# Graph layers on one core: the first unit's copies and scaling on VectorE, its row factors through the sums' banks, x loads behind the adjacency, and new order tables

## The chip, the cores and the metric

The kernel runs on one core of one Trainium2 chip. The metric is the time of one launch on the device, in microseconds. The profiler's span goes from the first to the last instruction of one profiled execution. In the text PE is TensorE, DVE is VectorE, ACT is ScalarE, POOL is GpSimd and SP is SyncE, which issues most of the DMAs.

## The reference, cut to what matters

There are eight batches of 2048 nodes with 128 features, all in float32, and one symmetric adjacency of 2048 x 2048 (about 3% of its entries are set). Each batch passes four layers, and each layer adds its result to x.

```python
h = maximum(layernorm(x), 0); x = x + L0(h)   # and so on for layers 1, 2, 3

# layers 0, 1, 3: graph attention, one head
Wh = h @ W.T                                  # layer 1: h @ W; layer 3: also a layernorm
e = leaky_relu(Wh @ a1 [:, None] + Wh @ a2 [None, :], 0.2)
out = softmax(where(adj > 0, e, -9e15)) @ Wh  # layers 0 and 3: elu at the end

# layer 2: attention of h with itself, four heads of 32
scores = leaky_relu(einsum('bihk,bjhk->bhij', x, x), 0.2)
out = softmax(where(adj == 0, -inf, scores)) @ x
```

## The kernel before, in words

A **unit** is one layer of one batch. Units of layers 0, 1 and 3 are of class `Gat`, those of layer 2 of class `Heads`. All units lie in one instruction stream, in which work of different batches alternates.

A `Gat` unit first makes its rows. The statistics are taken on DVE (L451; for the first unit L482), the reciprocal root by a power on POOL (L111; L488), a bias on DVE (L116; L492), and the scaled and clipped rows on ACT (L511), four quarters of 512 nodes each (q0 to q3). For each quarter PE transposes the rows (L540), ACT copies them out of PSUM (`copy`, L558), PE multiplies by the weights (`project`, L566), and ACT takes the exponentials (`exps`, L595 to L597) and multiplies four blocks by one of them (`put`, L591). The row factors `r` are needed along the free dimension on every partition. For the very first unit, batch 0's layer 0, and two more, `spread` turns them by eight transposes for each half (L650) into one PSUM pair, from where ACT copies them to SBUF (L659). For the other units they pass through DRAM: a turn on PE (L673), a copy, a write (L681) and a broadcast read (L698), both on SP's queue.

The softmax of such a unit is a chain of 32 **tokens**: two halves of its 2048 targets by sixteen blocks of sources. A token is one `front` on DVE (L718: the larger of two factors, times the adjacency) and one `back` on PE (L727: 8 blocks into PSUM, recorded as 16 matmuls). After 16 tokens `out` divides and adds the result to x. All tokens of all units form one chain in the order of the table TOKENS.

A `Heads` unit keeps its rows in DRAM in split form, and loads each head's sources `s`, targets `m` and values `v` (`load`, L928). It then runs 64 **beats**, 16 for each head. A beat is two score pairs on PE (L994), two exponentials on ACT (L1001), one mask on DVE (L1007) and its weighing on PE (L1016).

[...] Banks 4 to 7 are two **pairs**, which scores, transposes, projections and row turns borrow in turn; banks 1 to 3 hold the sums of the tokens (`sums`), and bank 0 the weighed values of the beats.

The adjacency (16 loads of 1 MB, `adjacency`, L366) becomes one byte per entry on DVE (L369, `edge`). `symmetry` (L382, L386 on PE and L392 on ACT) and `verdict` establish that it is symmetric; each of its pieces needs its row and the first unit's values. The loads use the tags `z` (five buffers) and `m` (two). `load_x` (L420) issues the loads of x on SP: batch 0's in four quarters, the others whole.

The order is not written by hand. Each step is an `add` with an engine, a duration, a due time and its needs. `Plan.run` goes through all of them with a model of the engines, and takes, of the steps that could start within WINDOW_US, the one due first; tokens' fronts are moved ahead by HURRY_US while more than one of their buffers is free. The due times come from TOKENS (start and step of each half), BEATS (start and step of each head), LEADS (how long before its start a unit is prepared) and EARLY (a shift for each kind of step). The model's durations affect only the order: each engine then works in that order, and waits for its data by semaphores.

Of the kernel before, what the change touches and what calls it, by code (L numbers as in the profile page):

```python
# [40 lines left out]
def adj_preln_d4(ctx: ExitStack, tc: tile.TileContext, x, adj, w0, a0, w1, a1, w3, a3,  # L41
# [117 lines left out]
    HURRY_US, WINDOW_US, BEAT_SUMS_US = 70.8, 0.139, 0.86  # L159

    EARLY = dict(front=-107.6, score=111.1, exp=-8.6, mask=-164.7, sums=-334.5)
# [78 lines left out]
    def fast(ctx):  # L240
# [117 lines left out]
        rows_in, squares = [], []  # L358

        def adjacency(j):  # L360
            tag, bufs = ("m", 2) if j % 6 > 3 else ("z", 5)
            raw = {}

            def load(op):
                raw[0] = big.tile([P, N], I32, tag=tag, name="raw", bufs=bufs)
                nc.sync.dma_start(out=raw[0], in_=adj[j * P:(j + 1) * P, :])  # L366

            def edges(op):
                nc.vector.tensor_scalar(edge[:, j, :], raw[0], 0.0, EDGE, op0=OP.is_gt, op1=OP.mult)  # L369

            last = add("SP", 2.5, 5.0 + 0.1 * j, load, takes=[tag], lag=5.5)
            rows_in.append(add("DVE", 1.14, 20.0 + 3.0 * j, edges, [last], frees=[(tag, last)]))
# [42 lines left out]
        def load_x(b, due):  # L415
            def load(op):
                X[b] = big.tile([P, NB, C], F32, tag="x", name="x", bufs=4)
                xv = x[b].rearrange("(n p) c -> p n c", p=P)
                for sl in ([slice(0, NB)] if b else [slice(q * 4, q * 4 + 4) for q in range(4)]):
                    nc.sync.dma_start(out=X[b][:, sl, :], in_=xv[:, sl, :])  # L420

            x_taken[b] = add("SP", 2.0, due, load, takes=["x"], lag=17.0 if b else 4.5)
            done[b, 0] = [x_taken[b]]
# [3 lines left out]
        class Unit:  # L427
# [44 lines left out]
            def first_moments(self):  # L472
# [22 lines left out]
                for half in range(2):  # L495
                    last = add("DVE", 1.9, half, lambda op, half=half: stats(op, half), self.after)
                    last = add("POOL", 3.4, half, lambda op, half=half: power(op, half), [last])
                    last = add("DVE", 0.09, half, lambda op, half=half: end(op, half), [last])
                    ready += [last] * 2
# [45 lines left out]
        class Gat(Unit):  # L545
            def beginning(self):
# [4 lines left out]
                ends, self.v_ready = [], []  # L551
                for q in range(4):
# [3 lines left out]
                    def copy(op, q=q, turn=turn):  # L556
                        self.h_t[q] = quarter("h_t")
                        nc.scalar.copy(self.h_t[q], ps[:, turn.got["pair"], :])  # L558

                    copied = add("ACT", 0.47, self.due(part), copy, [turn], frees=[("pair", turn)])  # L560

                    def project(op, q=q):
                        lo = op.got["pair"]
                        pv = ps[:, lo:lo + 2, :].rearrange("p b (k c) -> p (b k) c", c=256)
                        for k in range(4):
# [4 lines left out]
                                  takes=["pair"], frees=[("h_t", turn)])  # L570
                    put = self.put3 if layer == 3 else self.put
# [3 lines left out]
                self.v_ready = ends  # L575
# [8 lines left out]
            def put(self, q, lo):  # L584
# [4 lines left out]
                for k in range(4):  # L589
                    n = q * 4 + k  # L590
                    nc.scalar.activation(self.y[:, n, :C], pv[:, k, :C], AF.Copy, scale=self.y[:, n, C:CE])  # L591
# [46 lines left out]
            def spread(self):  # L638
# [4 lines left out]
                if (self.b, self.layer) in ((0, 0), (0, 1), (B - 1, 3)):  # L643
                    for half in range(2):
                        def turn(op, half=half):
                            lo = op.got["pair"]
                            pk = ps[:, lo:lo + 2, :].rearrange("p b (k t) -> p (b k) t", t=P)
                            for k in range(HB):
# [3 lines left out]
                        turned = add("PE", 0.9, self.due(0.95), turn,  # L652
                                     last if (self.b, self.layer) != (0, 0) else last[half * 2:half * 2 + 2],
                                     takes=["pair", "r"])

                        def copy(op, half=half, turned=turned):
                            self.r[half] = big.tile([P, HN], F32, tag="r", name="r", bufs=2)
                            lo = turned.got["pair"]
                            nc.scalar.copy(self.r[half], ps[:, lo:lo + 2, :].rearrange("p b t -> p (b t)"))  # L659

                        self.r_ready[half] = turned, add("ACT", 0.9, self.due(0.95), copy, [turned],
                                                         frees=[("pair", turned)])
# [28 lines left out]
            def targets(self, half, due):  # L691
# [9 lines left out]
                op = add("SP", 0.5, due, read, [self.written], takes=["r"], lag=7.5)  # L701
# [9 lines left out]
            def token(self, a, due, place, last_front, last_back, first, last, gate=None):  # L711
# [20 lines left out]
                powers = self.powers if self.layer == 3 else self.v_ready[jb // 4]  # L732
# [3 lines left out]
                b = add("PE", 1.8, due, back, [f, last_back, self.v_ready[jb // 4]],  # L736
# [149 lines left out]
        class Heads(Unit):  # L886
# [41 lines left out]
            def load(self, h, due):  # L928
# [7 lines left out]
                def target(op):  # L936
                    self.M[h] = m = big.tile([P, N], F32R, tag="m", name="m")
# [8 lines left out]
                s0 = add("SP", 1.9, due, lambda op: source(op, 0), self.there, takes=["s"], lag=3.0)  # L946
                m = add("SP", 1.0, due, target, self.there, takes=["m"], lag=7.0)
                s1 = add("SP", 1.9, due + 4, lambda op: source(op, 1), self.there, takes=["s"], lag=3.0)
                v = add("SP", 0.5, due, values, self.there, takes=["v"], lag=7.5)
                return s0, s1, m, v  # L950

            def beats(self, heads):
# [4 lines left out]
                for h, (start, step) in enumerate(heads):  # L957
                    ops = self.load(h, start - 24.0)
                    for jb in range(NB):
# [3 lines left out]
                        for c2 in range(2):  # L963
                            score = add("PE", 0.46, due - EARLY["score"] + c2, lambda op, s=s, c2=c2: self.scores(op, s, c2),
# [7 lines left out]
                        if jb == NB - 1:  # L972
                            score.frees.append(("m", ops[2]))
# [88 lines left out]
            (1, 0, 0): (-22.6, 16.91), (0, 1, 0): (53.7, 14.45), (0, 1, 1): (278.3, 12.5),  # L1062
            (1, 0, 1): (1550.7, 12.7), (2, 0, 0): (1538.2, 13.82), (2, 0, 1): (1781.1, 13.31),
            (1, 1, 0): (27.5, 13.73), (1, 1, 1): (467.0, 14.14), (2, 1, 0): (387.8, 14.31),
            (2, 1, 1): (552.8, 14.26), (3, 0, 0): (1505.8, 15.6), (3, 0, 1): (544.1, 12.33),
            (0, 3, 0): (1892.8, 13.82), (0, 3, 1): (1951.1, 14.82), (3, 1, 0): (2559.2, 13.34),
            (4, 0, 0): (1368.4, 13.75), (3, 1, 1): (1830.4, 13.22), (4, 0, 1): (1802.4, 13.44),
            (1, 3, 0): (1217.9, 11.81), (1, 3, 1): (1320.1, 15.08), (4, 1, 0): (1665.0, 14.27),
            (4, 1, 1): (2914.6, 13.92), (5, 0, 0): (1883.5, 13.18), (5, 0, 1): (1527.4, 14.37),
            (2, 3, 0): (1788.0, 14.72), (2, 3, 1): (2978.9, 11.74), (5, 1, 0): (3082.5, 14.35),  # L1070
            (5, 1, 1): (3404.4, 13.78), (6, 0, 0): (3203.1, 14.22), (6, 0, 1): (3460.2, 14.74),
            (3, 3, 0): (3608.3, 13.23), (3, 3, 1): (3684.5, 14.14), (6, 1, 0): (3899.4, 13.51),
            (6, 1, 1): (3952.0, 13.91), (7, 0, 0): (3923.9, 14.06), (7, 0, 1): (4831.6, 11.9),
            (4, 3, 0): (4281.7, 12.22), (7, 1, 0): (3732.3, 17.2), (7, 1, 1): (4400.2, 13.13),
            (4, 3, 1): (4958.4, 13.51), (5, 3, 0): (4812.0, 14.1), (5, 3, 1): (4921.6, 16.9),
            (6, 3, 0): (4366.7, 12.89), (6, 3, 1): (5490.0, 14.47), (7, 3, 0): (4783.0, 17.58),
            (7, 3, 1): (6177.5, 14.4),
        }
        BEATS = {
            (0, 0): (-186.75, 13.08), (0, 1): (-165.33, 21.31), (0, 2): (148.16, 8.98),  # L1080
            (0, 3): (258.71, 2.23), (1, 0): (-691.29, 9.57), (1, 1): (-490.1, 1.76),
            (1, 2): (-690.86, 3.48), (1, 3): (-210.23, 0.0), (2, 0): (88.81, 9.71),
            (2, 1): (97.72, 2.18), (2, 2): (646.55, 10.8), (2, 3): (1293.92, 18.43),
            (3, 0): (-837.42, 3.77), (3, 1): (1119.9, 1.12), (3, 2): (1122.42, 9.21),
            (3, 3): (1398.66, 23.92), (4, 0): (1467.16, 19.39), (4, 1): (2195.99, 8.65),
            (4, 2): (2652.74, 7.66), (4, 3): (3088.57, 11.55), (5, 0): (3462.55, 12.1),
            (5, 1): (3394.91, 8.46), (5, 2): (3605.57, 10.37), (5, 3): (3626.73, 12.28),
            (6, 0): (2736.83, 6.75), (6, 1): (3799.1, 0.43), (6, 2): (3983.93, 8.76),
            (6, 3): (3990.18, 12.29), (7, 0): (2647.8, 4.65), (7, 1): (2776.44, 0.0),
            (7, 2): (3122.04, 3.46), (7, 3): (3703.42, 8.07),  # L1090
        }
        LEADS = {
            (0, 0): 491.95, (1, 0): 357.11, (0, 1): 1280.8, (2, 0): 1208.77, (1, 1): 234.77,
            (3, 0): 828.81, (2, 1): 747.18, (0, 3): 274.58, (3, 1): 427.1, (4, 0): 119.58,
            (1, 3): 1195.59, (4, 1): 1350.06, (5, 0): 313.09, (2, 3): 599.37, (5, 1): 1322.07,
            (6, 0): 552.24, (3, 3): 361.02, (6, 1): 1007.92, (7, 0): 968.09, (4, 3): 325.57,
            (7, 1): 257.23, (5, 3): 781.66, (6, 3): 786.06, (7, 3): 1366.98, (0, 2): 836.12,
            (1, 2): 1588.43, (2, 2): 1046.3, (3, 2): -638.09, (4, 2): -597.43, (5, 2): 978.35,
            (6, 2): -1278.59, (7, 2): 69.8,
# [253 lines left out]
```

## Time and profile before

| | |
|---|---|
| median of 3 runs (lowest to highest) | 2748.1 us (2745.65 to 2750.09) |
| the profiled execution's own time | 2748.61 us |
| its span | 2746.8 us |
| mean granted PE clock in it | 0.993 |
| first adjacency conversion (L369), and the last | 14.38 us, 55.87 us |
| first token on PE (L727) | 35.86 us |
| first score on PE (L994) | 273.50 us |
| one front (L718), one mask (L1007), one exponential (L1001) | 1278, 2285, 1113 ns |

An engine's busy time is the sum of its recorded instructions. Matmuls are pipelined and their ends are modelled, so PE's busy time is no measure of how near it is to its peak; the distance from one start to the next in the timeline is. In a table of stretches the columns are PE, PE's weight loads, DVE, ACT and POOL, each with its count in brackets, then the granted clock, the DMA share and GB/s. In the waits, a line gives the waiting engine and line, what it waited for, the sum in microseconds, the number of times and the longest.

### The profile page before, as it was taken

The numbers are of one execution on the slowest core, as the hardware profiler recorded it, in microseconds if no ns is written. First come the engines' busy times: TensorE is split into PE (matmuls) and PEld (weight loads), VectorE is DVE, ScalarE is ACT, GpSimd is POOL, SyncE is SP. The second block draws the span as 40 slices with busy tenths as digits, with TensorE's granted clock in tenths as the row PEclk, the third lists the DMA queues.
The fourth block names the chain that finished last, engine by engine and source line by source line (L and its number), as shares of the span: only waits on it lengthen the run. The fifth ranks groups of instructions, "written<-read, shape, count | busy, mean of one in ns | idle before, by whom it ended". The sixth has DMA issues, their size and how long they took to land. (4 is left out here: it accounts for less than half of the span.)

```text
span 2746.8 us, 48941 instructions
## 1 busy us (share of the span) xinstructions
PE 2626.4 (96%) x20104; PEld 2020.1 (74%) x20104; DVE 2515.0 (92%) x3323; ACT 1720.2 (63%) x2789; POOL 261.7 (10%) x114
## 2 busy tenths in 40 slices
PE   6999999989998999999999999999999999999987
PEld 6999877757774777867777677786787667565677
DVE  7868899989999899999999999999999899899987
ACT  4333665576567558666767666665676757787651
POOL 2101010011000101111100110010111100011000
PEclk9999999999999999999999999999999999999999
DMA  8003223433323223232323321423225221422000
GB/s 311 17 9 99 64 55 62 93 85 62 62 47 77 55 55 85 55 70 55 67 62 81 78 47 47 103 53 70 55 59 105 47 58 28 108 54 55 13 16 25
DMA packets 212842, 181.80 MB, mean 66 GB/s; under 512 B 142448, under 2 KB 177728, under 8 KB 206464
## 3 DMA queue, kind: packets, MB, share of 16 engines
q1 hardware_dynamic: 144112, 156.46, 21.1%
q0 software_dynamic: 68080, 22.04, 8.0%
q8 instruction: 160, 2.62, 0.4%
q14 instruction: 74, 0.61, 0.1%
q10 hardware_dynamic: 416, 0.07, 0.0%
HBM read 123.03 MB, written 33.73 MB: 57 GB/s over the span
## 5 line engine op out<-in xcount | busy, mean ns | idle before, releaser
L1001 ACT ACTIVATE z<-ps,shift 128x1024 f32<-128x1024 f32 x1024 | 1122.7, 1113 | 727.1 <-PE ps L994 721.4
L727 PEld LDWEIGHTS ps<-y,zg 128*128 128x128 f32 x12288 | 1466.0, 192 | 71.3 <-DVE zg L718 20.0
L727 PE MATMUL ps<-y,zg 128*128 128x129 f32 x12288 | 1497.1, 276 | 15.5 <-DVE zg L718 10.4
L1007 DVE SCALAR_TENSOR_TENSOR z<-z,edge 128x2048 f32<-128x2048 f32 x512 | 1169.3, 2285 | 64.0 <-ACT z L1001 63.2
L718 DVE SCALAR_TENSOR_TENSOR zg<-r,cr,edge 128x1024 f32<-128x1024 f32 x768 | 970.5, 1278 | 98.1 <-PE ps L727 88.0
L994 PE MATMUL ps<-m,s 128*128 128x512 f32 x2048 | 721.1, 438 | 63.6 <-ACT z L1001 59.1
L994 PEld LDWEIGHTS ps<-m,s 128*128 128x128 f32 x2048 | 314.2, 191 | 339.4 <-ACT z L1001 241.1
L1016 PE MATMUL ps<-z,v 128*32 128x512 f32 x4096 | 500.9, 601 | 2.2 <-DVE z L1007 1.6
L1016 PEld LDWEIGHTS ps<-z,v 128*32 128x32 f32 x4096 | 103.5, 109 | 234.4 <-issue 183.3
L511 ACT ACTIVATE h<-x,nmrx,rstdx 128x128 f32<-128x128 f32 x512 | 210.7, 491 | 32.7 <-DVE nmrx L116 18.6
L111 POOL TENSOR_TENSOR rstdx<-varx,neg_half 128x16 f32<-128x16 f32 x31 | 130.3, 4204 | 643.9 <-DVE varx L106 643.9
L1041 POOL DMA_DIRECT2D x<-o x31 | 65.8, 2124 | 906.8 <-DVE o L1036 811.8
L451 DVE BATCH_NORM_STATS2 st<-x 128x6 f32<-128x128 f32 x496 | 106.2, 278 | 0.0
L566 PEld LDWEIGHTS ps<-rhs,h_t 128*128 128x128 f32 x768 | 98.3, 194 | 10.7 <-ACT h_t L558 3.0
L566 PE MATMUL ps<-rhs,h_t 128*128 128x130 f32 x768 | 104.3, 281 | 0.4 <-ACT h_t L558 0.3
L540 PE MATMUL ps<-ident,h 128*128 128x128 f32 x512 | 79.9, 279 | 15.7 <-ACT h L511 10.9
L795 POOL DMA_DIRECT2D x<-oa x26 | 23.4, 901 | 702.3 <-ACT z L1001 189.3
L540 PEld LDWEIGHTS ps<-ident,h 128*128 128x128 f32 x512 | 62.1, 142 | 35.0 <-ACT h L511 13.9
L760 DVE TENSOR_TENSOR oa<-ps,rs 128x384 f32<-128x384 f32 x144 | 73.9, 513 | 5.0
L558 ACT COPY h_t<-ps 128x512 f32<-128x512 f32 x96 | 55.2, 581 | 34.9 <-PE ps L540 34.9
L766 ACT ACTIVATE oe<-oa 128x1024 f32<-128x1024 f32 x32 | 33.8, 1058 | 68.8 <-DVE oa L785 59.2
L591 ACT ACTIVATE y<-ps,y 128x128 f32<-128x128 f32 x256 | 73.0, 369 | 0.0
(123 smaller groups left out, 830.7 us busy)
## 6 DMA issues: line engine op xcount, KB each, us to landing
s<-halves SPq DMA_DIRECT2D x256, 128.0 KB, 2.7
m<-halves SPq DMA_DIRECT2D x64, 512.0 KB, 6.5
r<-row SPq DMA_DIRECT2D x42, 512.0 KB, 3.7
raw<-in_adj_dram SPq DMA_DIRECT2D x16, 1024.0 KB, 16.9
x<-oa POOLq DMA_DIRECT2D x26, 512.0 KB, 4.6
values<-h SPq DMA_DIRECT2D x32, 256.0 KB, 2.2
halves<-hi SPq DMA_DIRECT2D x128, 64.0 KB, 1.7
halves<-lo SPq DMA_DIRECT2D x128, 64.0 KB, 1.7
```

What stands on the lines that cost most here:

```text
L111: nc.gpsimd.tensor_tensor(out=rstd, in0=v, in1=neg_half, op=OP.pow)
L451: nc.vector.bn_stats(out=key["st"][:, n, :], in_=rows()[:, n, :])
L511: nc.scalar.activation(self.h[q][:, k, :], X[self.b][:, n, :], AF.Relu, scale=key["rstd"][:, n:n + 1], bias=key["nmr"][:, n:n + 1])
L540: nc.tensor.transpose(pk[:, k, :], self.h[q][:, k, :], ident)
L566: nc.tensor.matmul(pv[:, k, :C + 2], lhsT=self.h_t[q][:, k * P:(k + 1) * P], rhs=rhs, start=True, stop=True)
L718: nc.vector.scalar_tensor_tensor(z, self.r[half], self.cr[:, 0, jb:jb + 1], edge[:, jb, half * HN:(half + 1) * HN], op0=OP.max, op1=OP.mult)
L727: nc.tensor.matmul(ps[:, self.banks(half, place)[i // 3], k * CE:(k + 1) * CE], lhsT=z[:, i * P:(i + 1) * P], rhs=self.y[:, jb, :], start= ...
L760: nc.vector.tensor_mul(key["a"][:, i0:i1, :], pv[:, :, :C], r[:, i0:i1, None].to_broadcast([P, i1 - i0, C]))
L994: nc.tensor.matmul(ps[:, lo + c, :], lhsT=self.S[h, jb // HB][:, at:at + P], rhs=self.M[h][:, (c2 * 2 + c) * 512:(c2 * 2 + c + 1) * 512], ...
L1001: nc.scalar.activation(self.z[s][:, c2 * HN:(c2 + 1) * HN], ps[:, lo:lo + 2, :].rearrange("p b t -> p (b t)"), AF.Exp, bias=shift)
L1007: nc.vector.scalar_tensor_tensor(self.z[s], self.z[s], 1.0, edge[:, jb, :], op0=OP.mult, op1=OP.mult, accum_out=self.den[:, h, jb:jb + 1])
L1016: nc.tensor.matmul(ps[c * HD:(c + 1) * HD, 0, :], lhsT=self.V[h][:, jb, :], rhs=z[:, c * 512:(c + 1) * 512], start=jb == 0, stop=jb == NB - 1,
```

## The change

For the first unit, batch 0's layer 0, the copies of the transposed rows out of PSUM and the multiplication of the four blocks of each quarter move from ACT to DVE; the multiplication is one instruction for a quarter instead of four. The transposes of its row factors need the exponentials only (`r_made`), no longer the scaled values, and half 0's go through banks 2 and 3 of the sums in place of a pair. The loads of x of the batches 1 to 7 need all adjacency loads in the plan, and so stand behind them on SP. In batch 0's layer 2, the targets of head 1 get a POOL instruction, `hold`, that reads an element of head 0's targets and writes one of head 1's, so that the load of head 1's targets comes after head 0's have landed. Several durations and lags of the model are altered, and TOKENS, BEATS, LEADS, EARLY, HURRY_US and WINDOW_US have new values. Of the sequence of TOKENS, the first eight halves differ in that batch 3's half 0 of layer 0 comes before batch 1's half 1 of layer 1; at the end both halves of batch 7's layer 1 come before batch 5's and 4's layer 3.

```diff
-    HURRY_US, WINDOW_US, BEAT_SUMS_US = 70.8, 0.139, 0.86
-    EARLY = dict(front=-107.6, score=111.1, exp=-8.6, mask=-164.7, sums=-334.5)
+    HURRY_US, WINDOW_US, BEAT_SUMS_US = 194.3, 0.136, 0.86
+    EARLY = dict(front=-260.8, score=238.0, exp=-105.8, mask=-318.7, sums=-441.8)
...
-            last = add("SP", 2.5, 5.0 + 0.1 * j, load, takes=[tag], lag=5.5)
+            last = add("SP", 2.5, 5.0 + 0.1 * j, load, takes=[tag], lag=6.0)
+            loaded.append(last)
...
-            x_taken[b] = add("SP", 2.0, due, load, takes=["x"], lag=17.0 if b else 4.5)
+            x_taken[b] = add("SP", 0.8 if b else 2.8, due, load, loaded[:] if b else (), takes=["x"], lag=17.0 if b else 3.5)
...
-                    last = add("POOL", 3.4, half, lambda op, half=half: power(op, half), [last])
+                    last = add("POOL", 1.7, half, lambda op, half=half: power(op, half), [last])
...
+                    begins = (self.b, layer) == (0, 0)
...
-                        nc.scalar.copy(self.h_t[q], ps[:, turn.got["pair"], :])
-                    copied = add("ACT", 0.47, self.due(part), copy, [turn], frees=[("pair", turn)])
+                        (nc.vector.tensor_copy if begins else nc.scalar.copy)(self.h_t[q], ps[:, turn.got["pair"], :])
+                    copied = add("DVE" if begins else "ACT", 0.61 if begins else 0.47, self.due(part), copy,
+                                 [turn], frees=[("pair", turn)])
...
+                    if begins:
+                        exped.append(add("ACT", 0.45, self.due(part + 0.04), lambda op, q=q, product=product:
+                                         self.put(q, product.got["pair"], False), [product] + exped[-1:]))
+                        ends.append(add("DVE", 0.75, self.due(part + 0.05), lambda op, q=q, product=product:
+                                        self.put_on_vector(q, product.got["pair"]), [exped[-1]],
+                                        frees=[("pair", product)]))
+                        continue
...
-                self.v_ready = ends
+                self.v_ready, self.r_made = ends, exped or ends
...
+            def put_on_vector(self, q, lo):
+                pv = ps[:, lo:lo + 2, :].rearrange("p b (k c) -> p (b k) c", c=256)
+                sl = slice(q * 4, q * 4 + 4)
+                nc.vector.tensor_mul(self.y[:, sl, :C], pv[:, :, :C], self.y[:, sl, C:CE].to_broadcast([P, 4, C]))
...
+                        room = "sums" if (self.b, self.layer, half) == (0, 0, 0) else "pair"
...
-                        turned = add("PE", 0.9, self.due(0.95), turn,
-                                     last if (self.b, self.layer) != (0, 0) else last[half * 2:half * 2 + 2],
-                                     takes=["pair", "r"])
+                        turned = add("PE", 0.9, self.due(0.95 if room == "pair" else 0.5), turn,
+                                     last if (self.b, self.layer) != (0, 0) else self.r_made[half * 2:half * 2 + 2],
+                                     takes=[room, "r"])
...
-                powers = self.powers if self.layer == 3 else self.v_ready[jb // 4]
+                powers = self.powers if self.layer == 3 else self.r_made[jb // 4]
...
-                b = add("PE", 1.8, due, back, [f, last_back, self.v_ready[jb // 4]],
+                b = add("PE", 1.785, due, back, [f, last_back, self.v_ready[jb // 4]],
...
+                if (self.b, h) == (0, 1):
+                    def hold(op):
+                        self.M[h] = big.tile([P, N], F32R, tag="m", name="m")
+                        nc.gpsimd.tensor_copy(self.M[h][0:1, 0:1], self.M[0].bitcast(F32)[0:1, 0:1])
+                    held = add("POOL", 1.0, due, hold, self.first_target, takes=["m"])
+                    self.there, there, m_taken = there + [held], there + [held], []
...
-                            score.frees.append(("m", ops[2]))
+                            score.frees.append(("m", ops[4]))
...
-            (1, 0, 0): (-22.6, 16.91), (0, 1, 0): (53.7, 14.45), (0, 1, 1): (278.3, 12.5),
+            (1, 0, 0): (-73.0, 12.4), (0, 1, 0): (287.7, 12.93), (0, 1, 1): (371.7, 10.73),
...
-            (0, 0): (-186.75, 13.08), (0, 1): (-165.33, 21.31), (0, 2): (148.16, 8.98),
-            (0, 3): (258.71, 2.23), (1, 0): (-691.29, 9.57), (1, 1): (-490.1, 1.76),
+            (0, 0): (-180.01, 6.53), (0, 1): (-578.0, 14.45), (0, 2): (-556.59, 10.52),
+            (0, 3): (-148.64, 9.04), (1, 0): (-1224.04, 11.55), (1, 1): (-933.99, 3.82),
...
-            (0, 0): 491.95, (1, 0): 357.11, (0, 1): 1280.8, (2, 0): 1208.77, (1, 1): 234.77,
+            (0, 0): 187.41, (1, 0): 971.94, (0, 1): 1566.41, (2, 0): 1305.46, (1, 1): 778.97,
```

The remaining entries of the three tables are altered in the same manner, and the model's lags of the reads of r (7.5 to 6.5), of m (7.0 to 7.5) and of v (7.5 to 5.5) and its durations of the loads of s (1.9 to 2.1) and of a score pair (0.46 to 0.455).

## The prediction

> **What bounds the kernel now.** I read the table of engines first, then busy time by stretch, the waits, and last the timeline of the places where the stretches show a loss. The table of engines:
>
> ```profile
> PE 2626.4 (96%) x20104; PEld 2020.1 (74%) x20104; DVE 2515.0 (92%) x3323; ACT 1720.2 (63%) x2789; POOL 261.7 (10%) x114
> ```
>
> TensorE is nearly always busy and VectorE is close behind: the kernel has two engines near their limit. A shorter time can only come from TensorE's idle time, 2746.8 - 2626.4 = 120 us, and each microsecond of it has a place. Busy time by stretch (PE first, then weight loads, DVE, ACT, POOL, granted clock, DMA share, GB/s):
>
> ```profile
> 0.00:36.00 36.00, 15.77 (x74) 11.43 (x75) 22.07 (x75) 18.98 (x60) 15.71 (x19) 1.00 0.93 365
> 36.00:60.00 24.00, 23.07 (x187) 22.44 (x188) 20.71 (x20) 11.57 (x43) 0.00 (x0) 0.93 0.97 340
> 60.00:270.00 210.00, 206.09 (x1846) 199.68 (x1845) 161.97 (x275) 69.84 (x207) 16.17 (x6) 1.00 0.14 37
> 270.00:2600.00 2330.00, 2261.78 (x17030) 1675.77 (x17029) 2193.43 (x2793) 1566.28 (x2367) 223.13 (x87) 1.00 0.31 64
> 2600.00:2670.00 70.00, 59.56 (x463) 51.54 (x461) 57.69 (x107) 36.45 (x80) 6.73 (x2) 0.93 0.05 16
> 2731.00:2747.00 16.00, 1.09 (x10) 0.90 (x9) 8.01 (x11) 2.11 (x2) 0.00 (x0) 0.67 0.13 38
> ```
>
> PE's idle time: 20.2 us before 36, 0.9 up to 60, 3.9 up to 270, 68.2 in the long middle, 10.4 up to 2670, and 15 behind the last token. The start and the middle are what this change touches. The start, from the timeline:
>
> ```profile
> 15.71 3.18 ACT L511 ACTIVATE h<-x,nmrx,rstdx 128x128 f32<-128x128 f32 x8 [12.56 <-DVE nmrx L492]
> 20.30 0.16 DVE L492 SCALAR_TENSOR_TENSOR nmrx<-varx,rstdx 128x8 f32<-128x8 f32 x1
> 22.23 1.14 ACT L591 ACTIVATE y<-ps,y 128x128 f32<-128x128 f32 x4
> 27.26 1.09 ACT L558 COPY h_t<-ps 128x512 f32<-128x512 f32 x2
> 33.50 0.99 ACT L659 COPY r<-ps 128x1024 f32<-128x1024 f32 x1
> 34.52 1.28 DVE L718 SCALAR_TENSOR_TENSOR zg<-r,cr,edge 128x1024 f32<-128x1024 f32 x1 [0.63 <-ACT r L659]
> 35.86 3.32 PE L727 MATMUL ps<-y,zg 128*128 128x129 f32 x16 [0.66 <-DVE zg L718]
> ```
>
> The first token (16 matmuls, L727) starts at 35.86, behind r's copy, which stands behind four quarters of rows, copies and scaling on ACT. For the middle, the waits of PE between 60 and 2600, and a stretch without tokens:
>
> ```profile
> PE ps L994 <- ACT z L1001: 59.1, 97, 2.4
> ...
> PE ps L994 <- DMA m<-halves: 1.8, 1, 1.8
> ```
> ```profile
> 575.09 0.73 PE L994 MATMUL ps<-m,s 128*128 128x512 f32 x2 [0.27 <-ACT z L1001]
> ...
> 579.55 0.72 PE L994 MATMUL ps<-m,s 128*128 128x512 f32 x2 [0.77 <-ACT z L1001]
> ...
> 584.55 0.27 PE L673 MATMUL ps<-ident,cr 128*16 128x128 f32 x1
> 585.92 0.74 PE L994 MATMUL ps<-m,s 128*128 128x512 f32 x2 [1.09 <-ACT z L1001]
> ```
>
> So 59 of the middle's 68 us are scores that wait for an exponential to empty a PSUM pair. They happen where no token is there to fill the gap, and most where a unit's own transposes or row turn have just borrowed one of the two pairs.
>
> [...] L727's mean is 276 ns, yet in the timeline tokens of 16 follow each other every 1.7 to 1.8 us, 112 ns each. So I count idle time and work moved, not busy shares. [...] the trace has 0.684 us (L914) and 0.692 (L1036) for the same size and source, which I use. [...] the trace shows 426 GB/s in 20 to 30 us, so a megabyte ahead of the adjacency costs it about 1.05/0.43 = 2.5 us.
>
> **The change, part by part.**
>
> (a) First unit's copies and scaling to VectorE. ACT loses 4 copies of 0.56 and 4 x 1.14 of scaling, 6.8 us; it keeps the exponentials, 3 of about 0.15. DVE gains 4 x 0.68 + 4 x 0.69 = 5.5 us, in a stretch where it is busy 22.1 of 36. It isn't free there: DVE takes its instructions in order, so a copy may sit behind an edge conversion (L369, 1.23 us) that waits for its rows.
>
> (b) The spread: half 0's transposes wait for the exponentials of q0 and q1 only, not for the scaling, and use two of the sums' banks, idle until the first token. That token needs r anyway, so no new wait is added; a pair is left for the projections.
>
> (c) Half 0's power is costed at 1.7, as it lasts (1.67 at 11.97); the bias (L492) came at 15.52 behind an edge conversion though the power ended at 13.64, and half 1's came at 20.30 though its power ended at 15.89. I expect about 13.8 and 16.1: 1.7 and 4.2 us earlier.
>
> (d) The x loads of later batches behind the adjacency. The fifth load at 0.8 (batch 1) moves, so rows land some 2.5 us earlier; batch 1's statistics (4 x 0.87 on DVE), its 3.8 us power on POOL and its first rows on ACT (1.65 at 31.95) leave the stretch before the first token. Each queue: on SP three loads stand after the sixteen adjacency loads. The last two already held SP from 37.5 to 55.8; behind them comes batch 1's row write, at 55.84 now and about 80 then, not late. On POOL nothing else waits. What is late next is batch 1: x lands about 60, its rows are made by about 80. The cover is the first unit's 32 tokens (57 us from about 26) with some 16 us of symmetry matmuls, enough until about 100; without that cover it would cost up to 10 us.
>
> First token, summed: bias 13.8; rows of q0 and q1, 2 x 1.65, to 17.2; turned 17.6; DVE copy 18.3; projection (0.9 to 1.05) 19.4; ACT busy with rows until 20.5, exponentials 20.9; eight transposes (0.92 to 1.2) 22.1; r copied (0.99) 23.2; front (1.28) 24.5. Two waits behind an edge conversion would add 2.4. I take 25.5, so 10 us earlier. Not all stays: while adjacency arrives DVE does an edge and a front in 2.5 us, and PE a token in 1.79. Batch 1's projections filled that gap (0.9 idle in 36 to 60); now symmetry matmuls must. I give back 2. **Start: -8 us**, between -12 and +1.
>
> (e) The one-element copy on POOL before head 1's target in the first batch. No row shows its wait. From above: it waits for head 0's target (6.5 us median, 7.9 longest landing), and what is queued behind it on POOL, a power or an add, makes one unit late by up to 8 us, under tokens. From below: head 0's load has the engines to itself, and PE's 1.8 us wait for m may go. I take 0. The other edits (lags, m freed by its taker, 1.785 for 1.8) change the order alone.
>
> (f) New tables: TOKENS, BEATS, LEADS, EARLY, HURRY_US. The work is the same, its order differs nearly everywhere; batch 3's layer 0 and batch 7's layer 1 come earlier. No row of before prices an order. From below: the clusters at 560:600 (8.0 us idle), 820:880 (11.1) and 2350:2380 (5.5) sum to 24.6; beyond them perhaps 45 of all 68 could go. From above: about 25 more. Better fitted durations and priorities chosen afresh speak for some gain. I take half the clusters and a little beside them: **-14 us**.
>
> Sum against the profiled execution: 2748.6 (span 2746.8 and 1.8 around it) - 8 - 14 = 2726.6, say **2727 us**. The median of the runs is 2748.1, half a microsecond away. One measurement of this kernel can tell about 0.2%, 5.5 us.
>
> **The rivals.**
> 1. The order does more: tokens stand beside beats everywhere, 40 of the 68 us go: 2748.6 - 8 - 40 = 2700. For it: neither engine is full in the clusters (DVE 31 of 40 us). Against it: DVE has 2193 of 2330 us in the middle, so other gaps may be VectorE's.
> 2. Only the start counts; the middle gives back what it saves, or a few us more: 2740 to 2752. For it: the start's account is long and plain. Against it: such a total rewrite of the order is unlikely to cancel to zero.
> 3. Slower: bare beats. Alone, a beat is set by VectorE's mask, 2285 ns and an 81 ns accumulator read, 2.37 us, where PE needs about 2.0 (two score pairs of 0.55 and half of 1.85 for weighing). Each beat without tokens loses 0.37 us. If the order bunches beats, the start's 8 us are gone from 22 more bare beats, and 2748.6 - 8 + 0.37 x 65 = 2765 with 65. It would sit in the middle, in L994's waits for ACT. For it: steps of 0.3 to 36 us in BEATS allow bunching. Against it: the old tables have the same spread.
> 4. The first token doesn't come earlier, as VectorE's in-order queue holds copies behind late rows: start 0, total 2735 with (f).
>
> **How the numbers follow.** The forecast with its near variants (rival 4 among them), 2712 to 2740: 0.45. Rival 1: 0.25. Rival 2: 0.14, of it 0.06 faster and 0.08 the same. Rival 3: 0.16. So faster 0.76, same 0.08, slower 0.16. The range, 2692 to 2757, takes in rival 1's place, rival 2 and the near part of rival 3.
>
> **What would show it.** Right: L558 and the new scaling on DVE in the first 25 us, a first token between 23 and 28, batch 1's statistics after 57; PE's idle time before the first 60 us near 13 instead of 21; L994's wait for ACT between 30 and 55 us. Wrong: a first token after 32; PE idle between 60 and 110 for batch 1; L994's wait above 75, which is rival 3; or a middle where PE waits for VectorE (L727 for zg) in place of ACT.

## The result, and the profile after

| | before | after |
|---|---|---|
| median of 6 runs each, side by side (lowest to highest) | 2749.1 us (2745.65 to 2755.53) | 2759.55 us (2758.7 to 2761.31) |
| the profiled execution, its span | 2748.61, 2746.8 us | 2759.1, 2757.3 us |
| first token on PE | 35.86 us | 29.58 us |
| token 16, token 32, token 128 on PE (counted from 0; token 32 is batch 1's first) | 75.9, 111.2, 349.2 us | 67.9, 118.2, 352.8 us |
| longest stretch between two tokens | 41 us, at 817 | 104 us, at 2115 |

The ratio is 1.0035, with an interval of 1.0022 to 1.0048: the changed kernel is slower by some 9.6 us. The forecast of 2727 us was wrong, in sign and in size. On other chips the kernel before had medians of 2751 to 2754 us, so below each run is given as its ratio to the kernel before on the same chip, with the 95% interval in brackets; 0.001 is 2.75 us. The table of engines after:

```profile
PE 2632.1 (95%) x20104; PEld 2021.0 (73%) x20104; DVE 2521.0 (91%) x3331; ACT 1712.4 (62%) x2769; POOL 256.0 (9%) x115
```

PE's busy time rose by 5.7 us though it has as many instructions (in a second profile of the changed kernel, by 2.9), and its idle time by 4.8, to 125.2. The stretches (columns as in the prediction) show where:

```profile
0.00:36.00 36.00, 21.59 (x107) 19.28 (x108) 26.85 (x68) 11.82 (x36) 12.34 (x18) 0.91 0.95 339
36.00:60.00 24.00, 24.00 (x226) 22.77 (x225) 22.32 (x20) 7.68 (x26) 0.00 (x0) 1.00 0.97 382
60.00:270.00 210.00, 198.55 (x1741) 192.81 (x1740) 157.91 (x280) 74.94 (x228) 19.14 (x7) 0.98 0.13 34
270.00:2600.00 2330.00, 2252.26 (x16899) 1660.08 (x16898) 2181.01 (x2789) 1562.22 (x2364) 216.80 (x88) 1.00 0.31 65
2600.00:2670.00 70.00, 67.04 (x556) 58.95 (x556) 66.89 (x104) 33.70 (x66) 7.69 (x2) 1.00 0.05 16
```

Up to 60 us PE is idle for 14.4 us in place of 21.2. But 60 to 270 now has 11.5 us of idle time in place of 3.9, and the middle 77.7 in place of 68.2; up to 2670 it is 3.0 in place of 10.4. The waits from 60 to 2600:

```profile
PE ps L1028 <- ACT z L1035: 62.1, 107, 2.4
PE ps L747 <- DVE zg L738: 9.6, 18, 1.7
PE ps L383 <- DVE plain L337: 4.1, 1, 4.1
```

Scores (L1028, before L994) wait for ACT about as long as before, 62.1 us against 59.1; the waits for VectorE have grown. Tokens' waits for fronts (L747 for zg) were, in the kernel before:

```profile
PE ps L727 <- DVE zg L718: 2.9, 6, 1.2
```

The start, as a timeline (L493 the bias, L570 the projection, L599 the scaling on DVE, L679 r's copy, L369 an edge conversion):

```profile
9.69 0.15 DVE L493 SCALAR_TENSOR_TENSOR nmrx<-varx,rstdx 128x8 f32<-128x8 f32 x1
...
16.92 2.10 PE L570 MATMUL ps<-rhs,h_t 128*128 128x130 f32 x8 [0.79 <-DVE h_t L561]
...
21.62 1.01 ACT L679 COPY r<-ps 128x1024 f32<-128x1024 f32 x1 [2.25 <-PE ps L670]
...
22.02 2.10 PE L570 MATMUL ps<-rhs,h_t 128*128 128x130 f32 x16
...
24.36 1.23 DVE L369 TENSOR_SCALAR edge<-raw 128x2048 uint8<-128x2048 int32 x1 [1.45 <-DMA raw<-in_adj_dram]
25.51 1.28 DVE L599 TENSOR_TENSOR y<-ps,y 128x512 f32<-128x512 f32 x2
...
26.77 1.23 DVE L369 TENSOR_SCALAR edge<-raw 128x2048 uint8<-128x2048 int32 x1
...
28.25 1.28 DVE L738 SCALAR_TENSOR_TENSOR zg<-r,cr,edge 128x1024 f32<-128x1024 f32 x1
```

r's first half is ready at 22.6, earlier than I worked out (23.2). The front stands behind two conversions and the scaling of two quarters on DVE, and starts at 28.25. At 74 us PE stops, here with DVE's own timeline beside it:

```profile
70.16 3.82 PE L747 MATMUL ps<-y,zg 128*128 128x129 f32 x32
78.12 0.37 PE L383 MATMUL ps<-edge,minus 128*128 128x256 fp8e4 x1 [4.14 <-DVE plain L337]
...
80.90 6.58 PE L747 MATMUL ps<-y,zg 128*128 128x129 f32 x32 [0.57 <-DVE zg L738]
```
```profile
67.98 1.29 DVE L738 SCALAR_TENSOR_TENSOR zg<-r,cr,edge 128x1024 f32<-128x1024 f32 x1 [0.28 <-PE ps L747]
...
69.32 6.28 DVE L452 BATCH_NORM_STATS2 st<-x 128x6 f32<-128x128 f32 x32
...
77.91 0.15 DVE L337 COPY plain<-ps 128x4 f32<-128x4 f32 x1
...
79.58 1.27 DVE L738 SCALAR_TENSOR_TENSOR zg<-r,cr,edge 128x1024 f32<-128x1024 f32 x1
```

Between two fronts lie 10 us, most of them statistics of two batches whose x came behind the adjacency. PE's next matmul (L383, of `symmetry`) waits for a copy (L337) that stands behind them on DVE, and the token for the front. After the stop, two tokens (32 matmuls) take 6.58 us instead of 3.82: the granted clock was at half for 10.2 us. In the records this begins at 76.40, some 2.4 us into a stop of 4.1. At 2168.77 another stretch at half clock, of 3.4 us, follows a stop of 2.4 us (from 2165.8); none follows one of 2.85 us (from 2638.56). In the kernel before, batch 1 was prepared (its turns from 34.5 to 48.3, its row turn at 53.2) while the adjacency came in; now its turns lie at 87 to 102 us.

The second place is the stretch without a token. The table TOKENS now has (7, 1, 0) directly behind (7, 0, 1), whose result it needs. The same 100 us, before and after:

```profile
2120.00:2220.00 100.00, 94.09 (x691) 65.84 (x690) 92.83 (x128) 66.08 (x106) 11.88 (x3) 1.00 0.18 38
```
```profile
2120.00:2220.00 100.00, 79.75 (x442) 36.29 (x442) 76.38 (x105) 90.93 (x151) 13.80 (x5) 0.98 0.35 69
```

PE is idle for 20 us in place of 6, and ACT is the busy engine. The first theory took these two places for the loss; the runs show that they are not, or not alone.

### The profile page after: what moved, and what is told of

Read it like the earlier page. It is cut to its first block, busy times and chain, and to the rows that moved or that the text cites. A ratio compares the mean times of both kernels' runs of the same rounds, so it can differ in the third digit from the quotient of the medians.

```text
span 2757.3 us, 48948 instructions
## 1 busy us (share of the span) xinstructions
PE 2632.1 (95%) x20104; PEld 2021.0 (73%) x20104; DVE 2521.0 (91%) x3331; ACT 1712.4 (62%) x2769; POOL 256.0 (9%) x115
## 5 line engine op out<-in xcount | busy, mean ns | idle before, releaser
L747 PEld LDWEIGHTS ps<-y,zg 128*128 128x128 f32 x12288 | 1462.7, 192 | 80.9 <-DVE zg L738 27.0
L747 PE MATMUL ps<-y,zg 128*128 128x129 f32 x12288 | 1496.3, 276 | 18.0 <-DVE zg L738 11.1
L1028 PE MATMUL ps<-m,s 128*128 128x512 f32 x2048 | 716.1, 436 | 65.5 <-ACT z L1035 62.1
L1028 PEld LDWEIGHTS ps<-m,s 128*128 128x128 f32 x2048 | 313.5, 190 | 339.0 <-ACT z L1035 250.4
L1050 PE MATMUL ps<-z,v 128*32 128x512 f32 x4096 | 503.0, 603 | 2.6 <-DVE z L1041 2.6
L1050 PEld LDWEIGHTS ps<-z,v 128*32 128x32 f32 x4096 | 103.9, 109 | 235.3 <-issue 189.5
L111 POOL TENSOR_TENSOR rstdx<-varx,neg_half 128x16 f32<-128x16 f32 x31 | 124.2, 4006 | 729.1 <-DVE varx L106 712.2
L570 PEld LDWEIGHTS ps<-rhs,h_t 128*128 128x128 f32 x768 | 99.7, 195 | 12.0 <-DVE h_t L561 2.6
L570 PE MATMUL ps<-rhs,h_t 128*128 128x130 f32 x768 | 105.1, 281 | 2.3 <-DVE h_t L561 1.9
L786 ACT ACTIVATE oe<-oa 128x1024 f32<-128x1024 f32 x32 | 33.9, 1061 | 62.1 <-DVE oa L805 56.4
```

The costliest lines, as they stand in the source:

```text
L111: nc.gpsimd.tensor_tensor(out=rstd, in0=v, in1=neg_half, op=OP.pow)
L570: nc.tensor.matmul(pv[:, k, :C + 2], lhsT=self.h_t[q][:, k * P:(k + 1) * P], rhs=rhs, start=True, stop=True)
L747: nc.tensor.matmul(ps[:, self.banks(half, place)[i // 3], k * CE:(k + 1) * CE], lhsT=z[:, i * P:(i + 1) * P], rhs=self.y[:, jb, :], start= ...
L1028: nc.tensor.matmul(ps[:, lo + c, :], lhsT=self.S[h, jb // HB][:, at:at + P], rhs=self.M[h][:, (c2 * 2 + c) * 512:(c2 * 2 + c + 1) * 512], ...
L1050: nc.tensor.matmul(ps[c * HD:(c + 1) * HD, 0, :], lhsT=self.V[h][:, jb, :], rhs=z[:, c * 512:(c + 1) * 512], start=jb == 0, stop=jb == NB - 1,
```

## The experiments

All runs compute the whole reference. For most the plan's order was written out and permuted, so that nothing else changes.

**The start alone.** In three runs some of the first 204 steps of the plan are permuted; in the fourth the first unit goes back to ScalarE.

```diff
         plan.run()
+        o = plan.order
+        o[48:73] = [o[i] for i in (61, 48, 49, 50, 51, 52, 65, 53, 54, 68,
...
```

> The changed kernel with its order kept, but for 25 steps at the start: the first two fronts and their tokens move ahead of edge conversions, scaling and the second weight matrix. Theory A (the start's gain was given back by VectorE's order, in which the first unit's fronts rank last): first front at about 23 us instead of 28.25, first token about 24.3 instead of 29.58; VectorE's own idle of 1.45 us at 22.9 is used, so 1 to 3 us less in all, 2756.5 to 2758.5. Theory B (the work moved to VectorE and the later x loads are themselves the cost): the first token comes earlier, but nothing is left of it at the end, 2759.5.

Measured: 1.0025 (1.0015 to 1.0035). The first token came at 24.4 us, but token 16 at 67.5 (67.9 in the changed kernel) and token 32 at 117.8. What is won at the first token is all but gone at token 16.

> The changed kernel with its order kept, but for 45 steps at 66 to 85 us of the plan: the statistics of batches 1, 2 and 3, which stand in one block on VectorE, alternate with the first unit's fronts. Theory A: TensorE's stop between 74 and 81 us goes, 5 to 6 us less, about 2754. Theory B: batch 1 is late because its x lands late, so its rows and its first token come no earlier and at most 2 us are gained, 2757.5 to 2759.5.

Measured: 1.0037 (1.0023 to 1.005). Batch 1's bias came later for the fronts let in between, and PE stopped at batch 1's turn instead, for 1.97 us, and at its projection for 3.21:

```profile
84.83 1.49 PE L541 MATMUL ps<-ident,h 128*128 128x128 f32 x4 [1.97 <-ACT h L512]
89.53 2.10 PE L570 MATMUL ps<-rhs,h_t 128*128 128x130 f32 x8 [3.21 <-ACT h_t L561]
```

> Both edits of e1 and e2 together. Theory A: the two add up, 7 to 8 us less than the changed kernel, about 2752, so that what remains against the kernel before, 3 us or so, lies in the middle. Theory B: 2757 to 2759.5.

Measured: 1.0038 (1.0024 to 1.0053), as the one before.

```diff
-                        (nc.vector.tensor_copy if begins else nc.scalar.copy)(self.h_t[q], ps[:, turn.got["pair"], :])
+                        nc.scalar.copy(self.h_t[q], ps[:, turn.got["pair"], :])
...
-                nc.vector.tensor_mul(self.y[:, sl, :C], pv[:, :, :C], self.y[:, sl, C:CE].to_broadcast([P, 4, C]))
+                for k in range(4):
+                    n = q * 4 + k
+                    nc.scalar.activation(self.y[:, n, :C], pv[:, k, :C], AF.Copy, scale=self.y[:, n, C:CE])
```

> The changed kernel with its order kept, but the first unit's four copies and its scaling (four instructions for a quarter again) run on ScalarE, at the same place in the order. Theory A: ScalarE is in the way of the row factors again, so the first token comes 1 to 3 us later and the total is 0 to 3 us longer, 2759.5 to 2762.5. Theory B: VectorE is freed of 5.5 us in a stretch that it bounds, so 2 to 5 us less, 2754.5 to 2757.5.

Measured: 1.0028 (1.0019 to 1.0037), first token at 30.4. The changed kernel itself had its first token at 29.6 in one profile and at 30.6 in another (of the control below), so in this order the move to VectorE shows no gain at the first token, and none at the end. The four ratios, 1.0025 to 1.0038, can't be told from the changed kernel's own, 1.0035 on the first chip and 1.0025 on that of the control.

**The two places again.** A control, batch 1's statistics put into VectorE's waits (steps 140 to 204 permuted), and the gap filled by putting (4, 3, 0) back between (7, 0, 1) and (7, 1, 0). With it the times of eight other half units of the tail and two leads are altered:

```diff
-            (7, 1, 0): (2989.3, 12.83), (7, 1, 1): (2119.2, 7.45), (5, 3, 0): (3315.8, 13.29),
+            (4, 3, 0): (3681.7, 12.22), (7, 1, 0): (3067.05, 12.83), (7, 1, 1): (4400.2, 13.13),
...
```

> The changed kernel itself, nothing altered, as a control on the chip of the three runs that follow. Every theory expects 1.0035 of the kernel before, 1.002 to 1.005 (some 9 us slower); the first token near 29.6 us, a stop of TensorE of some 7 us between 70 and 80 us with a stretch of half clock behind it, and 18 us of TensorE's idle time between 2150 and 2200 us.

Measured: 1.0025 (1.0015 to 1.0036).

> The changed kernel with the statistics of batch 1 issued on VectorE earlier (in its waits around 58 to 66 us, before 16 later fronts), those of batches 2 and 3 between fronts; all else in the same order. Theory A (the block of statistics at 69 to 79 us, and the half clock behind it, are the start's share of the loss): no stop of TensorE over 2 us between 70 and 95 us, no stretch of half clock of 10 us there, token 32 at some 110 us in place of 118, and 6 to 10 us off the changed kernel's time (2750 to 2754). Theory B (the start is bound by what one core can do by 110 us, whatever stands first; the loss is made in the middle): the stop moves or is paid elsewhere, within 3 us of the changed kernel. Theory C (the gap at 2115 to 2218 us takes up whatever is won ahead of it, since tokens alone fill it): token 32 earlier, the end within 3 us all the same.

Measured: 1.002 (1.0013 to 1.0027), 1.1 us below the control. The stop at 74 us is gone; another, 3.03 us up to 93.75, is left: the front stands behind a later batch's bias, which waits for its power on POOL. Token 32 came at 116.2. Theory A was right on the stop and wrong on its worth. B and C both expected an end within 3 us of the control; this run doesn't tell them apart.

> The changed kernel with the table of tokens altered in its tail alone: the half unit (4, 3, 0) stands between (7, 0, 1) and (7, 1, 0), as in the kernel before, so that tokens lie beside the attention of 2115 to 2218 us; the order up to about 2020 us is untouched. Theory C (the bare beats of that gap, some 17 us of TensorE's idle time against 2, are the loss that reaches the end): idle time between 2150 and 2200 us below 5 us, and 8 to 15 us off the changed kernel's time (2745 to 2751, the kernel before or better). Theory B' (tokens are conserved: those that fill the gap are missing later, in the last 300 us, and the planner's own sum is the same for both orders): the idle time moves past 2350 us, within 3 us of the changed kernel.

Measured: 1.0049 (1.0035 to 1.0062), slower than the control by 6.7 us. Idle time at 2120 to 2220 fell to 6.6 us, so the filling worked; theory C falls all the same. PE's waits from 2010 to 2700 show where it went. First the control, then the filled order:

```profile
PE ps L1028 <- ACT z L1035: 22.6, 43, 2.4
PE ps L747 <- DVE oa L780: 2.9, 1, 2.9
PE ps L1050 <- DVE z L1041: 2.6, 7, 0.7
PE ps L747 <- DVE rs L779: 2.6, 1, 2.6
...
PE ps L747 <- DVE zg L738: 0.4, 2, 0.3
```
```profile
PE ps L1028 <- ACT z L1035: 15.5, 27, 1.7
PE ps L747 <- DVE zg L738: 10.3, 5, 5.0
PE ps L1050 <- DVE z L1041: 6.0, 7, 1.4
PE ps L670 <- ACT cr L614: 3.4, 1, 3.4
```

Scores wait 7.1 us less for ACT. But tokens wait 10.3 us for VectorE's fronts in place of 5.9 for VectorE in all (three lines of L747), weighings (L1050) 3.4 us more for its masks, and a row turn (L670) 3.4: 11.2 us more against 7.1 less. The gap's wait went over from ACT to VectorE.

> Both alterations of the two runs before in one kernel: batch 1's statistics earlier and the half unit (4, 3, 0) in the gap. If both theories A and C hold, their gains add: 14 to 22 us off the changed kernel (2738 to 2746), faster than the kernel before by 3 to 11 us. If tokens are conserved, within 4 us of the better of the two runs.

Measured: 1.003 (1.0019 to 1.0041): 4.1 us better than the filled order alone, no better than the control.

**Orders exchanged.** Now the changed code follows a list, so that any stretch can have either kernel's order; these runs have no hold, and x[1] stands where the list puts it.

```diff
-        plan.run()
+        ORDER = (...) 
+        plan.follow(ORDER)
```

> The changed code of the first unit (copies and scaling on VectorE, row factors spread through the sums' banks) with every instruction issued in the order of the kernel before: x[1] is loaded ahead of the adjacency again, the tables and the hold of the second head have no effect. Theory O (the loss is one of order: x[1] behind the adjacency, and the new tables): no loss is left, 0.9985 to 1.0005 of the kernel before, token 32 at 110 to 113 us, batch 1's turns between 30 and 55 us. Rival U (the unit itself costs, since VectorE is what the start is bound by: 5 us more of its work): 1.002 or more.

Measured: 1.001 (1.000 to 1.002), between the two forecasts. In the old order the new unit's first token comes at 39.7, token 32 at 112.6 (before 111.2), batch 1 is ready in time.

> The changed code, the first 300 us in the order of the changed kernel (x[1] behind the adjacency, batch 1's statistics as one block), everything behind it in the order of the kernel before. Theory O in two parts: token 128 came 3.6 us later in the changed kernel, so the start is worth some 3 to 4 us and the new order behind it the other 6 to 7; then this kernel stands at 1.0005 to 1.002 of the kernel before. Rival S (the start is all of it, the later stretches only pass it on): 1.003 to 1.004. Rival T (the tables are all of it, later slack takes the start's loss up): 0.999 to 1.0005.

Measured: 1.0006 (0.9998 to 1.0015).

> The counterpart: the changed code, the first 300 us in the order of the kernel before (x[1] ahead of the adjacency, batch 1 prepared beside it), everything behind it in the order of the changed kernel, with its gap of 104 us without a token. Theory O in two parts: 1.0015 to 1.003 of the kernel before. Rival S: 0.999 to 1.0005. Rival T: 1.003 to 1.004.

Measured: 1.0042 (1.0029 to 1.0055). Rival T holds: with the same code, the changed kernel's order of the first 300 us costs nothing against the old one (1.0006 and 1.001), and its order behind 300 us costs 0.32%, some 9 us.

> The changed code in the order of the kernel before up to 2010 us, and behind that in the order of the changed kernel, with its gap of 104 us without a token and its own succession of the last ten half units. It splits the 8 us that the new order behind 300 us costs. By TensorE's idle time behind token 576 (68 us against 60), theory Q (the tail is most of it) expects 1.003 to 1.0045 of the kernel before; theory M (the stretch from 300 to 2010 us is most of it) 1.001 to 1.002.

Measured: 1.0031 (1.0022 to 1.0041).

> The counterpart: the changed code in the order of the changed kernel up to 2010 us (x[1] behind the adjacency), behind that in the order of the kernel before. Theory Q: 1.0005 to 1.002 of the kernel before. Theory M: 1.003 to 1.004.

Measured: 1.0006 (0.9998 to 1.0014). Theory Q holds: the order behind 2010 us costs 0.21%, some 6 us (1.0031 against 1.001 with the same start), the stretch from 300 to 2010 nothing by this pair (1.0006 here and with the old order from 300 us), up to 0.1% by the other (1.0042 and 1.0031, whose intervals overlap). A seam between two orders might cost something by itself; with the seam at the same place, the exchange in this direction lost nothing. PE's waits from 2010 to 2700, in the run of the unit alone and in the one with the changed tail:

```profile
PE ps L1034 <- ACT z L1041: 17.4, 28, 1.6
PE ps L767 <- DVE zg L758: 5.7, 2, 3.0
```
```profile
PE ps L1034 <- ACT z L1041: 24.1, 44, 2.4
PE ps L767 <- DVE oa L800: 2.9, 1, 2.9
PE ps L1056 <- DVE z L1047: 2.7, 7, 0.7
PE ps L767 <- DVE rs L799: 2.5, 1, 2.5
```

Scores wait 6.7 us longer for ACT, in 44 places instead of 28; tokens wait as long for VectorE as before, for other operations. Other waits (not shown) fell by some 3 us, so the waits tell only part of the 6 us.

**Orders found by search.** Neither order was made for a comparison of the code alone. So for each variant an order was sought by random moves, each kept or dropped by the planner's own sum with the changed kernel's prices.

> The changed code; the first 750 instructions of the plan (some 330 us) in an order found by a random search with the planner's own prices, x[1] ahead of the adjacency, everything behind in the order of the kernel before. The planner's sum falls by 8 to 9 us against the run of the unit alone. Theory E (the new first unit does have 8 us to give, if fronts stand first on VectorE and batch 1 is prepared beside the adjacency; the two orders tried so far each have one of the two): token 32 at 98 to 106 us, 0.9965 to 0.9985 of the kernel before. Rival (the start is bound by the adjacency's transfers and VectorE's work whatever the order): token 32 at 110 us or later, 0.9995 to 1.0015.

Measured: 0.9975 (0.9963 to 0.9988), first token at 32.6, token 32 at 109.6, token 128 at 340.8. The time is theory E's, the place isn't: by token 32 it had won only 1.6 us on the kernel before, and by token 128 8.4.

> The changed code, all 6263 instructions of the plan in an order found by such a random search, from the order of the kernel before; the planner's sum falls by 48 us. Theory O (the order of the instructions, not the first unit, is what this kernel's time turns on): a third to two thirds of that is seen, 0.986 to 0.995 of the kernel before. Rival L (the planner's sum says little of the chip: it put the changed kernel's plan level with the plan before, and was 10 us off): 0.997 to 1.005.

Measured: 0.9828 (0.9812 to 0.9844), 2705.18 us. Nearly all of the planner's 48 us are there.

> The code of the kernel before (its first unit with copies and scaling on ScalarE, row factors through a pair of banks), with the first 750 instructions of the plan in an order found by the same search as in the run with the searched start; behind that the order of the kernel before. Theory N (the gain of 0.25% seen there is the order's, the new first unit itself is worth nothing): 0.9965 to 0.9985 of the kernel before. Rival W (the new unit is what lets the start gain): 0.9995 or more.

Measured: 0.9962 (0.9948 to 0.9975), first token at 29.6 and token 32 at 105.6, with copies and scaling on ScalarE.

> The changed code with x[1] and all later x behind the adjacency, the first 750 instructions in an order found by the same search under that condition, the order of the kernel before behind them. Theory B (x[1]'s place in the queue is worth nothing by itself, only how the work around it is ordered): 0.9965 to 0.9985 of the kernel before. Rival P (batch 1's preparation behind the adjacency lies on the path, whatever the order): 0.999 to 1.001, token 32 at 113 us or later.

Measured: 0.9969 (0.9956 to 0.9981), token 32 at 111.9, token 128 at 342.8. Batch 1's turns lie at 81 to 96 us here too, and it costs nothing at the end.

> The code of the kernel before with all instructions of the plan in a searched order, from the order of the kernel before, by the same search and for as long as in the run with everything searched (0.983). Theory N: 0.981 to 0.986 of the kernel before, the same as with the changed code within 0.2%. Rival W (the new unit is worth its 6 to 8 us once the order fits it): 0.985 to 0.987.

Measured: 0.9796 (0.9779 to 0.9814), 2698.05 us against 2754.12: the fastest of all, 2% below the kernel before, with the old unit. Rival W falls. That the old unit came out 0.3% better isn't shown to be the unit's: one search was run for each, and the intervals touch. Its table of engines and its waits from 60 to 2600:

```profile
PE 2606.6 (97%) x20104; PEld 2022.6 (75%) x20104; DVE 2508.1 (93%) x3323; ACT 1719.9 (64%) x2789; POOL 263.1 (10%) x114
```
```profile
PE ps L1014 <- ACT z L1021: 19.7, 47, 0.8
PE ps L747 <- DVE zg L738: 9.9, 9, 3.6
PE ps L1036 <- DVE z L1027: 7.6, 13, 2.3
```

Two thirds of the scores' waits for ACT, 59.1 us in the kernel before, are gone with the same work on each engine. PE's waits for VectorE's fronts and masks grew, from 3.4 us to 17.5, so its idle time fell by less, from 120.4 us to 91.0. The other 19.8 us of the shorter span are PE's busy time, nearly all in the scores, of which there are as many as before (busy time, mean of one in ns, and idle time ahead; first the kernel before):

```profile
L994 PE MATMUL ps<-m,s 128*128 128x512 f32 x2048 | 721.1, 438 | 63.6 <-ACT z L1001 59.1
```
```profile
L1014 PE MATMUL ps<-m,s 128*128 128x512 f32 x2048 | 702.7, 434 | 28.2 <-ACT z L1021 19.7
```

## Why the prediction was wrong, point by point

- **"A shorter time can only come from TensorE's idle time"** failed as a bound. The fastest run has 29.4 us less of idle time and 19.8 less of busy time with the same 20104 matmuls; of the changed kernel's 10.5 us of longer span, 5.7 are busy time.
- **(a)** Right in size: the eight DVE instructions take 5.5 us, four of 0.686 and four of 0.684; the 0.684 (L914) and 0.692 (L1036) that I took are VectorE's reads of 512 elements from PSUM in the kernel before. Its worth was not: with the unit on ScalarE the changed order has its first token within what two profiles of the changed kernel differ by, and the same end, and with a searched start the two units are level.
- **(b), (c)** Right in direction. VectorE's order was in the way in the kernel before: it stood idle for 1.04 and 1.22 us ahead of the edge conversions at 16.71 and 19.16, while half 1's bias, whose power ended at 15.89, came behind them at 20.30. The biases came at 9.69 and 12.10, not 13.8 and 16.1, and r's half at 22.6. That this lies so near to 23.2 is luck: the first bias came 4.1 us earlier than I summed, and the way from it to r took 12.9 us in place of 9.4. Part of that is a price: I took 0.9 to 1.05 us for a projection of eight matmuls, as later ones cost, but at 13.19 and 16.92 it took 2.10 us (sixteen took 2.10 at 22.02).
- **First token at 25.5.** It was 29.58: two conversions and two scalings ahead of the front where I had allowed for two waits of 1.2. The rank of fronts in the plan, not data, put them there, as the run with the fronts moved ahead shows (24.4).
- **(d), the cover "enough until about 100"**, failed first. I checked that PE had tokens for batch 1's delay, and forgot that the tokens come through VectorE, on which the delayed statistics stand in one block; the stop of 4.1 us was the result, with 10.2 us at half clock behind it. Yet its removal gave 1.1 us, which the intervals don't tell from nothing, and x[1] behind the adjacency costs nothing in a fitting order.
- **"Start: -8 us"** failed as a term. The first token was 6.3 us earlier and token 16 8 us, but token 32 came 7 us later and token 128 3.6. (Of the 7 us, 4.5 are the place of symmetry matmuls that the changed order puts just ahead of token 32; the token before it came 2.6 us later, at 111.4.) I took the first token for the path. Work that the kernel before did beside the adjacency (batch 1's four turns and projections, its statistics) was moved behind it, and the gain repaid that; measured with equal code, the two starts are level (1.0006, 1.001).
- **(e)** No run tests the hold alone. PE's wait for m from 60 to 2600 went from 1.8 to 1.1 us.
- **(f), "-14 us" for the tables**, is the step that fails most: they cost some 6 to 9 us, most of it behind 2010 us. I had no row that priced an order, and took half of what could be gained as likely. That there was much more to gain was right: the searched orders took 46 and 56 us. The planner's own sum, which is no measurement, would have shown the cost: the old order with the new prices (above all a token at 1.785 in place of 1.8 and a score pair at 0.455 in place of 0.46) ends at 2773 us, the changed one at 2782. With each kernel's own prices they look level, 2781 and 2782. My reading of the scores' waits, that most stand behind a unit's transposes or row turn, was wrong too: counted over the trace of the kernel before, 24 of the 59 us have such a use of a pair within the 5 us ahead.
- **Rival 3** ended near the time (2765), and its place, bare beats, is there: a stretch of 104 us with PE idle for 20. But the sign I gave for it, scores waiting over 75 us for ACT, was not (62.1), and filling the stretch made the kernel slower. So bare beats mark this tail, and are not shown to be its cause. Which of the tail's tables makes it slower, the sequence or the beats' due times, stays open; the filled order has the old sequence there, and is no better.

## What to carry to other kernels

An earlier first result is worth nothing by itself: follow the gain to the next stage's first result (token 16, 32, 128 here), and ask of work that is moved which engine it displaces, not only whether its consumer has other work. When code and an order come together, exchange them one at a time before judging either; here the code was worth nothing that could be measured, the order cost some 9 us, and better orders of the old code gave 56. Compare two plans only with the same prices.

## What the runs showed that was not expected

- A stop of PE of 4.1 us in the records was followed by 10.2 us at half clock, in which two tokens took 6.58 us in place of 3.82. In the kernel before, 10.2 us at half clock (from 2630.55) followed a stop of 3.0 us (at 2626.6). So busy time grew without an instruction more, but it is a small part of the 5.7 us: the half clock lasted 44.4 us in all in the changed kernel and 39.8 in the one before, half of whose difference gives an estimate of at most 2.3 us.
- With nothing but the order changed, PE's waits for ACT's exponentials fell from 59.1 to 19.7 us, with ACT as busy as before (1719.9 us against 1720.2): most of a wait that looked like a bound of two PSUM pairs was one of order.
